# Attention's queries of two heads from seven products of quarters, with h and its sums reloaded for each group

## The chip, the cores and the metric

The kernel runs on one core of a Trainium2 chip. A core has five engines with queues of their own, each worked off strictly in order: TensorE (PE for the matmuls, PEld for its weight loads), VectorE (DVE), ScalarE (ACT), GpSimd (POOL) and SyncE (SP), which here only issues DMAs. POOL and ACT issue some too. The metric is the device time of one execution in microseconds; the lower, the better. The kernel before took 2233.8 us, the median of three runs (2233.77 to 2240.36).

## The reference

Four rows (batch entries) of 512 tokens with 512 channels pass through two layers. The first is a gated recurrence followed by Mamba-2, and another such gate followed by a mixture of experts. The second, in which the change lies, is a gate followed by grouped-query attention, and a last gate followed by a gated FFN:

```python
x = x + _L1_attn_ref(_L1_cond_ref(x, fside, fside, L1_cond_w, L1_cond_u, cond), w_q, w_kv, w_dense)
x = x + _L1_ffn_ref(_L1_cond2_ref(x, fside, fside, L1_cond2_w, L1_cond2_u, cond), ...)
```

```python
HEADS, GROUPS, KVC = (16, 4, 128)      # 4 heads to a group, HPG = 4
q = einsum('bsh,he->bse', x, w_q).reshape(b, sq, GROUPS, HPG, KVC)
kv = einsum('bsh,he->bse', x, w_kv)
k, v = split(kv, 2, axis=-1)           # each (b, sk, GROUPS, KVC)
scores = einsum('bqgpd,bkgd->bgqpk', q, k) * KVC ** -0.5
probs = softmax(where(causal, scores, -inf))
ctx = einsum('bgqpk,bkgd->bqgpd', probs, v).reshape(b, sq, HEADS * KVC)
return einsum('bse,eh->bsh', ctx, w_dense)
```

All of it is in float32. Here x is the gated input, h in the kernel.

## The kernel before, in words

**Layout.** Activations are kept transposed: channels on the 128 partitions, tokens along the free axis. h of one row is a tile of 128 x 4 x 512 floats (1 MB): four blocks of 128 channels, 512 tokens. A float32 product of 128 x 128 weights with 512 columns stands in the profile as two MATMUL records with two LDWEIGHTS.

**Stages.** In the order of time: the first layer's recurrence and Mamba-2, the mixture of experts (to about 1117 us of the profiled execution), attention (to about 1995 us), the FFN to the end.

**Attention.** The loop at the end of the attention block runs over `heads_`: for each of 4 groups, for each of 4 rows, 4 heads; 64 heads in all. `begin(n + 1)` makes the next head's queries one step ahead. For the first head of a group and row it also calls `start_group`, which makes kT (`pk`, L1630) and v (`pv`, L1638). Then `scores` makes the current head's four blocks of causal scores (`psc`, L1674). DVE masks them and takes the maximum, ACT takes the exponential (L128), DVE normalises (L1686) and transposes within blocks of 32 (L1690). Four POOL DMAs send the result to DRAM (`turned`, L1698) and one fetches it back turned (`pT`, L1716). Three heads later `settle` calls `context` (`pctx`, L1742), and after the fourth head of a row `dense` (`pd`, L1757), which DVE adds to x (L1765).

**Queries.** `queries(u, i)` is one head: four products accumulate over the four blocks of channels, and ACT scales the result into qT:

```python
pq = ps_tp("pq")
for k in range(NC):
    nc.tensor.matmul(pq, lhsT=u.wq[:, k, i * KVC : (i + 1) * KVC], rhs=u.h[:, k, :],
                     start=(k == 0), stop=(k == NC - 1))
qT = sm.tile([P, T], F32, tag="qT", name="qT")
nc.scalar.mul(qT, pq, SCALE)
```

The PSUM tag "tp" has two banks. `wq` of a group (1 MB) is loaded by `load_group` into one of two buffers; the first h (`early_h`) is made in the other one during the mixture of experts, and copied to its own place by L1617.

**h.** The four rows' h stay in SBUF for all four groups, in the four buffers of tag "h" of pool `gp`. While group 0 runs, the h of the following row is made at the third head of each row: `load_results` (`rr`, L1508, on SP) and `combine` (L1515 on ACT, L1516 on DVE, `pcb` L1521 on PE, L1525 on DVE) finish x of that row; `gated` loads the gate (L417, 1 MB) and multiplies (L406). After attention, `gated_halves` makes the FFN's h in the same buffers and splits it into a high and a low part (L1858 on ACT, L1859 on DVE). The FFN's first products (`pfg`, `pfu`, L1872 and L1873) read these.

**Other work in attention.** `nudge` spreads the last gates' recurrence (`make_gates`: `kt`, `ek`, `ekv`, scans, `eu`) over the heads, on DVE and ACT. Its loads go through SP's queue.

**Order.** A list scheduler in the programming layer sorts the instructions of all engines by its own estimates, within the program's dependencies. The queues are then fixed, and on the chip an instruction that waits holds up everything behind it on its engine. A DMA waits on its issuing engine's queue. Pools with `reuse_waits="tile"` let a new tile in old memory wait for the last user of just the tiles that lay there.

Of the kernel before, what the change touches and what calls it, by code (L numbers as in the profile page):

```python
# [10 lines left out]
F32 = mybir.dt.float32  # L11
# [72 lines left out]
def block_kernel(ctx: ExitStack, tc: tile.TileContext, a: dict, out: bass.AP):  # L84
# [61 lines left out]
    def ps_tp(name):  # L146
        return ps.tile([P, 512], F32, tag="tp", name=name, bufs=2)
# [1338 lines left out]

    def load_group(g):

        wq = wa.tile([P, NC, HPG * KVC], F32, tag="wq", name="wq")
        w = HPG * KVC  # L1490
        nc.sync.dma_start(
            out=wq, in_=a["w_q"][:, g * w : (g + 1) * w].rearrange("(k p) m -> p k m", p=P)
        )
        wkv = wa.tile([P, 2, NC, KVC], F32, tag="wkv", name="wkv")
        for i in range(2):
            c0 = i * GROUPS * KVC + g * KVC
            nc.sync.dma_start(
                out=wkv[:, i], in_=a["w_kv"][:, c0 : c0 + KVC].rearrange("(k p) m -> p k m", p=P)
            )
        return wq, wkv  # L1500

    def load_results(b, t, queue):

# [35 lines left out]
    with tc.tile_pool(name="moe_w2", bufs=1, reuse_waits="tile") as wm:  # L1539
# [18 lines left out]
        order_blocks(NEARLY, NBLK)  # L1558
        moe.know(ALWAYS)
        more(NBLK - 8)  # L1560
        first_group = load_group(0)

        more(NEARLY + FIRST + 2)
        results = {t: load_results(0, t, nc.gpsimd) for t in range(2)}
# [6 lines left out]
                results[t + 2] = load_results(0, t + 2, nc.gpsimd)  # L1571
        assert moe.i == ALWAYS + 2
        n = len(nc.cur_bb.bb.instructions)
        early_h = gated(2, 0, x[0], wa, tag="wq", name="h2_0")
        early_th = [
            i for i in nc.cur_bb.bb.instructions[n:] if i.engine == nc.scalar.engine
        ]
# [7 lines left out]


    right = dict(side="right", reuse_waits="tile")
    gp = ctx.enter_context(tc.tile_pool(name="gates", bufs=4, **right))
    with att as ph:
        wdp = ph.enter_context(tc.tile_pool(name="att_wd", bufs=1, **right))  # L1590
        sm = ph.enter_context(tc.tile_pool(name="att", bufs=2, **right))
        mp = ph.enter_context(tc.tile_pool(name="att_m", bufs=1, **right))
# [20 lines left out]
                nc.gpsimd.memset(blocks[:, :, lo:hi, :], 0.0)  # L1613
        turned_d = [dr.tile([QUAD, SQ, QUAD, SLOTS * SQ], F32, name=f"turned{i}") for i in range(4)]

        hs = [gp.tile([P, NC, T], F32, tag="h", name="h2")] + [None] * (B - 1)
        nc.sync.dma_start(out=hs[0], in_=early_h)  # L1617

        class Group:
            pass  # L1620
# [1 line left out]
        def start_group(g, b, w):  # L1622
            u = Group()
            u.g, u.b, u.ctxT = g, b, []
            u.last_row = g == GROUPS - 1 and b == B - 1
            u.wq, wkv = w
            u.h = h = early_h if (g, b) == (0, 0) else hs[b]
            pk = ps_mm("pk")
            for k in range(NC):
                nc.tensor.matmul(  # L1630
                    pk, lhsT=wkv[:, 0, k, :], rhs=h[:, k, :], start=(k == 0), stop=(k == NC - 1)
                )
            u.kT = sm.tile([P, T], F32, tag="kT", name="kT")
            nc.scalar.copy(u.kT, pk)
            pv = ps_mm("pv")
            for t in range(NT):
                for k in range(NC):
                    nc.tensor.matmul(  # L1638
                        pv[:, t * P : (t + 1) * P],
                        lhsT=h[:, k, t * P : (t + 1) * P],  # L1640
                        rhs=wkv[:, 1, k, :],
                        start=(k == 0),
                        stop=(k == NC - 1),
                    )
            u.v = sm.tile([P, NT, KVC], F32, tag="v", name="v")
            nc.scalar.copy(u.v.rearrange("p t d -> p (t d)"), pv)
            return u

        def queries(u, i):
            pq = ps_tp("pq")  # L1650
            for k in range(NC):
                nc.tensor.matmul(  # L1652
                    pq,
                    lhsT=u.wq[:, k, i * KVC : (i + 1) * KVC],
                    rhs=u.h[:, k, :],
                    start=(k == 0),
                    stop=(k == NC - 1),
                )
            qT = sm.tile([P, T], F32, tag="qT", name="qT")
            nc.scalar.mul(qT, pq, SCALE)  # L1660
            return qT

        def scores(u, i, qT):

# [109 lines left out]
                dense(old)  # L1774

        weights, dense_w = {0: first_group}, {0: load_dense(0)}
        heads_ = [(g, b, i) for g in range(GROUPS) for b in range(B) for i in range(HPG)]

        def begin(n):
            g, b, i = heads_[n]  # L1780
            if i == 0:
                if b == 0 and g + 1 < GROUPS:
                    weights[g + 1] = load_group(g + 1)
                groups[g, b] = start_group(g, b, weights[g])
            return groups[g, b], queries(groups[g, b], i)


        ffg_d = dr.tile([C, INTER], F32, name="ffg_d")
# [4 lines left out]
                es.enter_context(tc.issue_after(th))  # L1793
            act.use(act.LOG_EXP)
        look_ahead(1, (0, 1))
        groups = {}
        numbers = iter(range(GROUPS * B * HPG))
        ready, held = begin(0), []
        for n, (g, b, i) in enumerate(heads_):
            u, qT = ready  # L1800
            if g == 0 and i == 0 and b + 1 < B:
# [8 lines left out]
                nc.sync.dma_start(out=to, in_=a[name])  # L1810
            if g and b == 0 and i == 3:
                dense_w[g] = load_dense(g)
            if n + 1 < len(heads_):
                ready = begin(n + 1)
            if g == 0 and i == 2 and b + 1 < B:
                act.use(act.EXP)
                hs[b + 1] = gated(2, b + 1, x[b + 1], gp, tag="h", name=f"h2_{b + 1}")
                act.use(act.LOG_EXP)
            prs = scores(u, i, qT)
            held.append((u, prs))  # L1820
            if len(held) > 3:
                settle()
# [10 lines left out]
            act.use(act.SILU)  # L1833


    LOW = 0xFFF
    cuts = (0, 3 * P, INTER)

# [204 lines left out]
```

## Time and profile before

| | |
|---|---|
| median of three runs | 2233.8 us |
| profiled execution | 2242.7 us, span 2241.0 us, granted clock 0.981 |
| PE busy | 2135.2 us, 95% |
| DVE, ACT, POOL busy | 1526.2, 968.9, 455.8 us |
| queries `pq` on PE, 512 records | 237.4 us |
| ACT `qT` (L1660), 64 of 593 ns | 38.0 us |
| DMA | 357.38 MB, 159 GB/s on average |

A group's line in the profile gives line, engine, operation, what is written and read, the shapes and the number of instructions; then the busy time in us, the mean length of one in ns, and the engine's idle time just before them, with what ended most of it. Matmuls are pipelined, so the mean length of one (599 ns) is more than the distance from one to the next. In the timeline a line is a run of like instructions: start, length, engine, line, tiles, shapes, count, and in brackets the idle time before it with what ended that. In the view by windows each engine has its busy time and the number of instructions; the granted clock of PE (1.00 is full), the DMA engines' mean share and the GB/s follow.

### The profile page before, as it was taken

How to read it: one execution, taken by the hardware profiler on the slowest of the kernel's cores; microseconds unless marked ns; L12 is line 12 of the kernel's file. 1: busy time of each engine (PE TensorE's matmuls, PEld its weight loads, DVE VectorE, ACT ScalarE, POOL GpSimd, SP SyncE). 2: the span in 40 equal slices, each digit the busy share in tenths (PEclk: the TensorE clock that was granted, in tenths of full speed). 3: DMA queues.
4: the chain of work that ended last, by engine and by line, in shares of the span. 5: the costliest groups of instructions: out<-in, count | busy, mean ns of one | idle time of the engine just before them, and what ended most of it. 6: DMA issues, size and time to landing. Idle time of an engine off the chain costs nothing.

```text
span 2241.0 us, 23830 instructions
## 1 busy us (share of the span) xinstructions
PE 2135.2 (95%) x7570; PEld 1224.9 (55%) x7570; DVE 1526.2 (68%) x3039; ACT 968.9 (43%) x1899; POOL 455.8 (20%) x620
## 2 busy tenths in 40 slices
PE   4979999999999999999998999999999999999998
PEld 2545565565665444444454455555555555568887
DVE  8799889989653566676477766677767765555332
ACT  4576776765732234333254333333334432333221
POOL 4023242422222111222211111112112122100000
PEclk9989999999999999999989999999999999999999
DMA  7542341432424458988676555555645464531100
GB/s 257 195 132 73 107 155 67 156 122 67 167 83 141 152 190 285 382 289 285 211 252 195 179 183 150 160 164 181 185 140 175 141 195 140 185 122 38 38 20 20
DMA packets 112452, 357.38 MB, mean 159 GB/s; under 512 B 14592, under 2 KB 23168, under 8 KB 102912
## 3 DMA queue, kind: packets, MB, share of 16 engines
q1 hardware_dynamic: 78656, 224.43, 29.0%
q0 software_dynamic: 31360, 127.16, 18.9%
q10 hardware_dynamic: 2304, 4.20, 0.5%
q8 instruction: 62, 1.02, 0.2%
q14 instruction: 70, 0.57, 0.1%
HBM read 337.91 MB, written 108.00 MB: 199 GB/s over the span
## 4 chain that ended last, share of the span: by engine, by line
PE 40%; DVE 8%; ACT 1%; DMA 1%; issue 0%; DVEq 0%; ACTq 0%
PE pd L1757 10%; PE pq L1652 6%; PE pctx L1742 4%; PE psc L1674 4%; PE pk L1630 3%; PE pv L1638 3%; PE pfo L1873 2%; PE pfo L1872 2%; PE pfg L1872 2%; PE pfg L1873 2%; PE pfu L1872 2%; PE pfu L1873 2%; DVE nmax L1679 1%; DVE turned L1690 1%; DVE pr L1686 1%; DVE psc L1677 1%
## 5 line engine op out<-in xcount | busy, mean ns | idle before, releaser
L1698 POOL DMA_DIRECT2D turned<-turned x248 | 136.0, 555 | 622.8 <-DVE turned L1690 387.9
L128 ACT ACTIVATE pr<-psc,nmax 128x128 f32<-128x128 f32 (+3 forms) x256 | 134.7, 527 | 286.9 <-DVE nmax L1679 284.2
L1652 PE MATMUL pq<-h,wq 128*128 128x512 f32 x512 | 237.4, 599 | 1.8 <-DVE h L406 1.2
L1757 PE MATMUL pd<-cx,wd 128*128 128x512 f32 x512 | 222.4, 592 | 0.0
L1765 DVE TENSOR_TENSOR xr<-xr,pd 128x512 f32<-128x512 f32 x64 | 44.0, 687 | 196.8 <-PE pd L1757 196.8
L1674 PE MATMUL psc<-kT,qT 128*128 128x128 f32 (+3 forms) x512 | 160.0, 442 | 15.5 <-ACT pr L128 14.4
L1757 PEld LDWEIGHTS pd<-cx,wd 128*128 128x128 f32 x512 | 96.1, 190 | 114.8 <-issue 110.3
L1057 PE MATMUL pc<-h,wxb 128*128 128x512 f32 x320 | 145.6, 610 | 6.6 <-DVE h L406 4.0
L1652 PEld LDWEIGHTS pq<-h,wq 128*128 128x128 f32 x512 | 94.7, 193 | 102.2 <-issue 90.8
L1742 PE MATMUL pctx<-pT,v 128*128 128x512 f32 (+3 forms) x512 | 148.4, 433 | 0.0
L1742 PEld LDWEIGHTS pctx<-pT,v 128*128 128x128 f32 x512 | 96.7, 190 | 76.2 <-issue 50.5
L847 PE MATMUL po<-w,yT 128*128 128x512 f32 x296 | 134.2, 593 | 0.6 <-DMA w<-in_w2x 0.4
L814 PE MATMUL pg<-w,hT 128*128 128x512 f32 x296 | 134.2, 594 | 0.0
L825 PE MATMUL pn<-w,hT 128*128 128x512 f32 x296 | 133.4, 593 | 0.7 <-DMA w<-in_w1x 0.7
L1674 PEld LDWEIGHTS psc<-kT,qT 128*128 128x128 f32 x512 | 84.9, 191 | 74.2 <-ACT pr L128 29.7
L1679 DVE TENSOR_REDUCE nmax<-psc 128x1 f32<-128x128 f32 (+3 forms) x256 | 122.1, 481 | 2.1
L1690 DVE STREAM_TRANSPOSE turned<-pr 128x128 f32<-128x128 f32 x248 | 117.0, 493 | 1.2
L1128 PE MATMUL pz<-wzt,h 128*128 128x512 f32 x256 | 116.6, 605 | 0.3 <-ACT st L1229 0.3
L1276 PE MATMUL po<-wot,yT 128*128 128x512 f32 x256 | 115.4, 605 | 0.0
L1057 PEld LDWEIGHTS pc<-h,wxb 128*128 128x128 f32 x320 | 60.8, 195 | 78.0 <-issue 71.5
L1686 DVE TENSOR_SCALAR pr<-pr,rsum 128x128 f32<-128x128 f32 (+3 forms) x256 | 95.7, 375 | 2.2
L1677 DVE TENSOR_TENSOR psc<-psc,mask 128x128 f32<-128x128 f32 x256 | 70.9, 284 | 37.4 <-PE psc L1674 37.0
(348 smaller groups left out, 4186.3 us busy)
## 6 DMA issues: line engine op xcount, KB each, us to landing
w<-in_w1x SPq DMA_DIRECT2D x76, 1024.0 KB
turned<-turned POOLq DMA_DIRECT2D x248, 208.0 KB, 3.8
pT<-turned POOLq DMA_DIRECT2D x62, 832.0 KB, 7.3
w<-in_w2x SPq DMA_DIRECT2D x38, 1024.0 KB
wb<-in_b1x SPq DMA_DIRECT2D x38, 512.0 KB
lm<-cs SPq DMA_DIRECT2D x32, 512.0 KB
kt<-in_fT SPq DMA_DIRECT2D x62, 256.0 KB
ek<-ek SPq DMA_DIRECT2D x62, 256.0 KB
```

The source lines that it names most:

```text
L128: nc.scalar.activation(*args, **kw)
L814: nc.tensor.matmul(pg, lhsT=hT[:, k, :], rhs=self.w1[s][0][:, k, :], start=(k == 0), stop=(k == NC - 1))
L1057: nc.tensor.matmul(pc, lhsT=wxb[:, k, m * P : (m + 1) * P], rhs=h[:, k, :], start=(k == 0), stop=(k == NC - 1),)
L1652: nc.tensor.matmul(pq, lhsT=u.wq[:, k, i * KVC : (i + 1) * KVC], rhs=u.h[:, k, :], start=(k == 0), stop=(k == NC - 1),)
L1674: nc.tensor.matmul(psc[:, :n], lhsT=qT[:, qi * P : n], rhs=u.kT[:, :n], start=True, stop=True)
L1679: nc.vector.tensor_reduce(nmax, psc[:, :n], AX.X, ALU.max, negate=True)
L1690: nc.vector.transpose(blocks[:, :, 3 * qi : 4 * qi + 1, :].rearrange("p c k j -> p k c j"), pr)
L1698: nc.gpsimd.dma_start(out=d[:, :, r].rearrange("c i s -> i c s"), in_=blocks[r * SQ : (r + 1) * SQ].rearrange("i c k j -> i c (k j)"),)
L1742: nc.tensor.matmul(pctx[:, kj * P :].rearrange("p (q r j) -> p q r j", r=QUAD, j=SQ), lhsT=u.v[:, kj, :], rhs=pT[:, :, 4 * kj : 10 + kj : ...
L1757: nc.tensor.matmul(po, lhsT=dense_w[u.g][:, i, m * P : (m + 1) * P], rhs=u.ctxT[i], start=(i == 0), stop=(i == HPG - 1),)
L1872: nc.tensor.matmul(out_, lhsT=w, rhs=xs[0], start=first_, stop=False)
L1873: nc.tensor.matmul(out_, lhsT=w, rhs=xs[1], start=False, stop=last_)
```

## The change

The queries of two heads are one product of a 2 x 2 arrangement of quarters. The weights' quarters a11, a12, a21, a22 are (two blocks of channels) x (one head's 128 columns); h's quarters b11, b12, b21, b22 are (two blocks of channels) x (256 tokens); the result's quarters are (one head) x (256 tokens). Instead of eight products of quarters there are seven (p1 to p7), of four sums of weight quarters (s1 to s4, on POOL after each load) and four sums of h quarters (t1 to t4, on DVE, once for each row, tile `ht`, 1 MB). A product of quarters is two matmuls of 256 columns, so a pair of heads takes 14 of these in place of 8 of 512 columns. The results are put together by five DVE operations, two scalings on ACT and two sums on POOL, 256 columns each. One product (p3) and its DVE operation are issued after the current head's scores.

h and ht of each row are stored to DRAM in group 0 and loaded again for every group, h into two buffers, ht into one. The weights are loaded by pairs of heads (`load_pair`), one buffer for the first and one for the second pair, raw weights and sums side by side; `early_h` now takes the second pair's buffer. Pool `gp` is opened after attention instead of before it, and attention's h has a pool `hp` of its own in that place.

```diff
 def load_group(g):
-    wq = wa.tile([P, NC, HPG * KVC], F32, tag="wq", name="wq")
-    w = HPG * KVC
-    nc.sync.dma_start(out=wq, in_=a["w_q"][:, g * w : (g + 1) * w].rearrange("(k p) m -> p k m", p=P))
...
+def load_pair(g, j):
+    w = wa.tile([P, 2, NC, 2 * KVC], F32, tag=f"wq{j}", name=f"wq{j}", bufs=1)
+    c0 = (g * HPG + 2 * j) * KVC
+    nc.sync.dma_start(out=w[:, 0], in_=a["w_q"][:, c0 : c0 + 2 * KVC].rearrange("(k p) m -> p k m", p=P))
+    quads = w.rearrange("p s k (h m) -> p s k h m", h=2)
+    a11, a12, a21, a22 = (quads[:, 0, 2 * c : 2 * c + 2, h] for h in range(2) for c in range(2))
+    s1, s2, s3, s4 = (w[:, 1, i].rearrange("p (c m) -> p c m", c=2) for i in range(4))
+    nc.gpsimd.tensor_tensor(s1, a21, a22, ALU.add)
+    nc.gpsimd.tensor_tensor(s3, a11, a21, ALU.subtract)
+    nc.gpsimd.tensor_tensor(s2, s1, a11, ALU.subtract)
+    nc.gpsimd.tensor_tensor(s4, a12, s2, ALU.subtract)
+    return a11, a12, a22, s1, s2, s3, s4
...
-    early_h = gated(2, 0, x[0], wa, tag="wq", name="h2_0")
+    early_h = gated(2, 0, x[0], wa, tag="wq1", name="h2_0", bufs=1)
...
-gp = ctx.enter_context(tc.tile_pool(name="gates", bufs=4, **right))
 with att as ph:
+    hp = ph.enter_context(tc.tile_pool(name="att_h", bufs=1, **right))
...
-    hs = [gp.tile([P, NC, T], F32, tag="h", name="h2")] + [None] * (B - 1)
-    nc.sync.dma_start(out=hs[0], in_=early_h)
+    HT = T // 2
+    h_d = [dr.tile([P, NC, T], F32, name=f"h_d{b}") for b in range(B)]
+    t_d = [dr.tile([P, 4, 2, HT], F32, name=f"t_d{b}") for b in range(B)]
+    def row_tiles(b):
+        return (hp.tile([P, NC, T], F32, tag="h", name=f"h2_{b}", bufs=2),
+                hp.tile([P, 4, 2, HT], F32, tag="ht", name=f"ht_{b}"))
...
+    def mix(h, ht):
+        b11, b12, b21, b22 = quarters(h)
+        t1, t2, t3, t4 = (ht[:, i] for i in range(4))
+        nc.vector.tensor_tensor(t1, b12, b11, ALU.subtract)
+        nc.vector.tensor_tensor(t2, b22, t1, ALU.subtract)
+        nc.vector.tensor_tensor(t3, b22, b12, ALU.subtract)
+        nc.vector.tensor_tensor(t4, t2, b21, ALU.subtract)
+    def keep_row(b, h, ht):
+        nc.sync.dma_start(out=h_d[b], in_=h)
+        nc.sync.dma_start(out=t_d[b], in_=ht)
+    def load_row(b):
+        h, ht = row_tiles(b)
+        nc.sync.dma_start(out=h, in_=h_d[b])
+        nc.sync.dma_start(out=ht, in_=t_d[b])
+        return h, ht
...
-    def queries(u, i):
+    def queries(u, j):
...
+        x1, y5, u2, u3, u4 = (both(v) for v in ("x1", "y5", "u2", "u3", "u4"))   # 256 columns, one buffer each
+        p1, p6 = two()                       # two() is one bank of tag "tp", cut in halves
+        product(p1, a11, b11)
+        nc.scalar.mul(x1, p1, SCALE)
+        product(p6, s2, t2)
+        plus(u2, p6, x1)                     # DVE: SCALE * p6 + x1
+        p2, p7 = two()
+        product(p2, a12, b21)
+        plus(q[0][:, lo], p2, x1)
+        product(p7, s3, t3)
+        plus(u3, p7, u2)
+        p5, p4 = two()
+        product(p5, s1, t1)
+        nc.scalar.mul(y5, p5, SCALE)
+        product(p4, a22, t4)
+        nc.gpsimd.tensor_tensor(u4, y5, u2, ALU.add)
+        nc.gpsimd.tensor_tensor(q[1][:, hi], y5, u3, ALU.add)
+        plus(q[1][:, lo], p4, u3, -1.0)
+        yield q
+        p3, _ = two()
+        product(p3, s4, b22)
+        plus(q[0][:, hi], p3, u4)
+        yield
...
         if g == 0 and i == 2 and b + 1 < B:
-            hs[b + 1] = gated(2, b + 1, x[b + 1], gp, tag="h", name=f"h2_{b + 1}")
+            h = gated(2, b + 1, x[b + 1], hp, tag="h", name=f"h2_{b + 1}", bufs=2)
+            ht = hp.tile([P, 4, 2, HT], F32, tag="ht", name=f"ht_{b + 1}")
+            mix(h, ht)
+            keep_row(b + 1, h, ht)
+            at_hand[g, b + 1] = h, ht
+        elif i == 2 and (g, b) != (GROUPS - 1, B - 1):
+            to_g, to_b = heads_[n + HPG][:2]
+            at_hand[to_g, to_b] = load_row(to_b)
+        if b == B - 1 and i == 1 and g + 1 < GROUPS:
+            pairs_w[g + 1, 0] = load_pair(g + 1, 0)
         prs = scores(u, i, qT)
+        end_queries()                        # p3 of the pair just made
...
+gp = ctx.enter_context(tc.tile_pool(name="gates", bufs=4, **right))   # after attention
```

## The prediction

> **What bounds the kernel now.** I read the page first: engine shares, the slices in time, the costliest groups.
>
> ```profile
> span 2241.0 us, 23830 instructions
> ...
> PE 2135.2 (95%) x7570; PEld 1224.9 (55%) x7570; DVE 1526.2 (68%) x3039; ACT 968.9 (43%) x1899; POOL 455.8 (20%) x620
> ...
> L1652 PE MATMUL pq<-h,wq 128*128 128x512 f32 x512 | 237.4, 599 | 1.8 <-DVE h L406 1.2
> ...
> turned<-turned POOLq DMA_DIRECT2D x248, 208.0 KB, 3.8
> pT<-turned POOLq DMA_DIRECT2D x62, 832.0 KB, 7.3
> ```
>
> PE is the bound; the queries (pq) hold 237 us of it. The last two lines give what a DMA takes from issue to landing by size.
>
> Then the busy time by window: two short stretches just after PE had stood still, and the steady part of attention.
>
> ```profile
> 1120.00:1126.00 6.00, 5.85 (x8) 2.48 (x8) 1.99 (x3) 2.48 (x3) 0.71 (x4) 0.52 0.75 284
> 1158.00:1164.00 6.00, 5.20 (x7) 2.23 (x8) 6.00 (x14) 4.66 (x10) 2.75 (x5) 0.56 0.81 223
> 1187.00:1800.00 613.00, 603.35 (x1957) 324.26 (x1957) 446.71 (x1143) 244.76 (x584) 128.67 (x235) 1.00 0.57 171
> ```
>
> The pairs are busy us and instructions of PE, PEld, DVE, ACT, POOL; then granted clock, DMA share, GB/s. From 1187 to 1800 us PE is idle 1.6%, DVE 27%: whatever PE saves there is saved, and whatever it waits there is lost.
>
> Last, the timeline of PE: rates, the start of attention, its end.
>
> ```profile
> 1117.16 0.63 PE L1521 MATMUL pcb<-ident,rr 128*128 128x128 f32 x4 [1.53 <-DVE rr L1516]
> 1120.15 6.44 PE L1630 MATMUL pk<-h,wkv 128*128 128x512 f32 x8 [2.37 <-DVEq L1579]
> 1126.43 3.73 PE L1638 MATMUL pv<-wkv,h 128*128 128x128 f32 x32
> ...
> 1275.73 2.32 PE L1742 MATMUL pctx<-pT,v 128*128 128x512 f32 x8
> ...
> 1277.89 13.90 PE L1757 MATMUL pd<-cx,wd 128*128 128x512 f32 x32
> ...
> 1981.23 13.90 PE L1757 MATMUL pd<-cx,wd 128*128 128x512 f32 x32
> 1994.57 0.80 PE L1873 MATMUL pfu<-h_lo,ffu 128*128 128x512 f32 x1
> ```
>
> A record is half a product (each product makes two). 32 records of 512 columns take 13.90 us, 0.429 each; 32 of 128 take 3.73 us, 0.112 each. Between them a 256-column record costs 0.2175; the pctx line (two each of 512, 384, 256 and 128) fits that: 2.16 us plus a tail. The eight pk records after 1.53 and 2.37 us of idleness took 6.44 instead of 3.6 us: the granted clock was 0.52. At the end, dense (pd) and FFN follow without a gap.
>
> **The change, part by part.**
>
> *PE work.* Out: 512 records x 0.429 = 219.6 us. In: 32 pairs x 14 products x 2 = 896 records x 0.2175 = 194.9. Gain 25 us; ends 27 (0.2145, half of 0.429) and 22.
>
> *Waits for ht.* ht (1 MB, one buffer) is reloaded for 12 of the 16 rows. In the built program SP's load of the next ht waits for the last product of the row's second pair that reads the old one; PE's queue, which is in order, holds the next row's first ht product soon after. I priced the PE work between the two by the rates above: 2.37 us in six rows, 3.66 in two, 4.52 in four; together 39.6 us. No row gives the landing of this load. Nearest: in the trace the packets of h<-g, the same size on the same queue, ended 4.4 (quiet queues) to 6.4 us after issue; by the two POOL lines above 5.6 us per MB more than 208 KB, 8.3 us. I take 6.2 with the wake-ups (attention's DMA share is 0.57): 12 x 6.2 - 39.6 = 35 us. Ends: 4.7 (4.4 and the wake-ups) gives 17, 8.3 gives 60. Behind the waiting product stand the same head's third and fourth scores, then pctx and pd, so DVE and ACT run dry too and nothing makes it good.
>
> The Trainium skill (DMA: Bandwidth & Descriptors, Anatomy of one DMA) fits 2.0 us plus bytes at 436 GB/s, by which 1 MB would be 4.4 us and this term some 17 us; only the quietest load of this trace agrees, the loads in attention took 5.3 to 6.4.
>
> *Clock after the waits.* In the trace of before, after its first 30 us, PE has nine gaps of 2.4 us or more at full clock; after seven the granted clock fell to 0.5, for 3.4 us at least; of six gaps of 1.8 to 2.0 us, after four. The waits above are 1.7 to 3.8 us. A drop costs half its length, less what falls into the gap: 12 x 0.75 x 2.1 = 19 us. Ends 7 (a third of them, 1.7 each) and 41 (all, 3.4 each).
>
> The Trainium skill (TensorE: Matmul & The Clock Gate, Part 1) wants a whole idle window of about 3.4 us before the gate closes. Here 1.9 us sufficed before 1156 us. By the page only the six longest waits would count and this term would be about 10 us.
>
> *Entrance to the FFN.* Pool gp, opened after attention now, shares memory with attention's; the load of h3_0 waits for the very last pd product. Before, it was issued at 1790 us. So PE stands from the end of pd: load 4.4 to 5.5, first chunk's h 0.69 (L406), its cast 0.61 (L1858), wake-ups: 6.6 us; then PE starts at half clock and DVE feeds it (8 operations of 0.69). I take 10; ends 6.5 and 14.
>
> *Start of attention.* early_h sits in the second pair's buffer (wq1). wq1's load so waits until row 0's pk, pv and all seven products are done, 1130.0 + 28 x 0.2175 = 1136; on SP's queue, in order, three of the four rr loads of row 1 stand behind it (issued from 1122.9 before, first used by ACT at 1130.7). They land about 10 us late, and the h of row 1 with them. Ahead of them SP also waits for the SBUF copy of h (about 6 us) before h_d can be stored. wq1 lands near 1142 and its four sums on POOL (0.71 each, half of L1223's 1.43 for 512 elements) end near 1145, when the second pair could start. Of the 10 us, PE has two longer query groups (2.4 us each) as cover: I take 8; ends 0 and 14 (all of it, and a drop of the clock).
>
> *Putting quarters together.* No row has the operation. DVE: between 0.415 (L1679, 256 columns) and 0.687 (L1765, 512): 5 x 32 x 0.42 = 67 us, and 16 sums of h at 0.69, 11 us; DVE goes from 73% to about 82% in attention, below PE. ACT: 38.0 us out, 64 x 0.43 in. POOL: 64 sums of queries and 32 of weights x 0.71 = 68 us, from 21% to 29%; the scheduler put them between the DMA issues of turned, heads ahead of use. On the path: the third bank's products wait for the evacuation of the first (x1 on ACT, then u2 on DVE), with 2 to 3 us of other PE work between; where DVE is in a softmax, part shows. 32 x 0.2 = 6 us; ends 0 and 20 (one DVE operation and its queue, 0.6). If that cover goes, each pair pays 0.6.
>
> *Sums of h in group 0.* For rows 1 to 3 DVE cannot write ht until the old one is read, 2.1 us for the three sums before the first product, under 3.9 to 28 us of PE work: 3 us; ends 0 and 8.
>
> *SP and memory.* 24 loads and 8 stores of 1 MB more, and four more weight loads: 36 more issues. 32 MB over 880 us is 36 GB/s beside 171: hidden while the DMA share is 0.57; if not, the landing time above grows. The loads of h have two buffers, a row of notice: nothing. The first pair's POOL sums end before attention: nothing, else up to 3 us.
>
> Sum: -25 + 35 + 19 + 10 + 8 + 6 + 3 = +56 us on an execution of 2242.7 us (span 2241.0). It is 0.4% above the median of the runs, 2233.8; I put the same difference on the median: 2290.
>
> **Rivals.** Within 0.3% (6.7 us) nothing can be told from no change.
>
> *A. The ht loads land under cover* (ends not slower). It needs a landing within 2.4 to 4.5 us of the last read. For it: the scheduler placed the products there. Against: 208 KB took 3.8 us, and no 1 MB load less than 4.4. Waits and clock drops (54 us) go: 2290 - 54 = 2236; with the start hidden too, about 2225. It decides from landings below about 4 us.
>
> *B. Loads land as late as pT*: 60 us of waits, 30 of clock: 2290 + 36 = 2326. For it: the load of the next h is issued right behind, and pT shares the engines. Against: h<-g.
>
> *C. DVE becomes the second bound*: with 82% busy in order, each pair's evacuations cost 0.6 to 1 us: 2290 + 20 = 2310. For it: DVE is 100% busy in 1158 to 1164. Against: 73% from 1187 on.
>
> *D. The sums are not seven products*: the order of the built program shows 14 half-size products a pair, so no.
>
> **How the numbers follow.** Forecast 0.58, B 0.17, C 0.10, A 0.15 (of it 0.10 below -0.3%, 0.05 within). The forecast's own range, from the ends that are likely together (waits 25 to 45, clock 10 to 30): 2262 to 2318. For 8 in 10 I reach half into A and to the middle of B: 2240 to 2328. Faster 0.10, same 0.05, slower 0.85.
>
> **What would show it.** PE's waits in groups 1 to 3: twelve, for ht, 1.7 to 4 us each, 25 to 45 us together; a granted clock below 1.0 after most; pq records of 256 columns near 0.2175 us; one PE gap of 6 to 8 us before the first pfg; rr and h of row 1 about 10 us later. It is wrong if attention has no DMA waits on PE (then A), or if pq waits for DVE more than for DMA (C).

## The result and the profile after

The changed kernel takes 2404.4 us (median of six runs, 2396.8 to 2409.3) against 2237.5 us for the kernel before: a ratio of 1.0745, 95% interval 1.0722 to 1.0768. The direction was forecast, the size was not: 167 us more, where 56 were worked out and the range ended at 2328.

The page of the changed kernel: span, busy time, the products of the queries by what they read, and the two transfers by size.

```profile
span 2403.0 us, 25117 instructions
...
PE 2174.0 (90%) x7954; PEld 1322.4 (55%) x7954; DVE 1598.4 (67%) x3216; ACT 958.3 (40%) x1898; POOL 530.8 (22%) x716
...
L1712 PE MATMUL pq<-ht,wq 128*128 128x256 f32 x512 | 138.1, 411 | 55.3 <-DMA ht<-t_d 42.6
...
L1712 PE MATMUL pq<-h,wq 128*128 128x256 f32 x384 | 102.3, 395 | 5.8 <-DVE h L406 2.9
...
turned<-turned POOLq DMA_DIRECT2D x248, 208.0 KB, 3.9
pT<-turned POOLq DMA_DIRECT2D x62, 832.0 KB, 7.4
```

PE went from 95 to 90% busy. The two transfers land as before. The same stretch of attention as in the view by windows of before:

```profile
1187.00:1800.00 613.00, 524.99 (x1820) 323.70 (x1820) 407.46 (x1036) 197.08 (x478) 145.65 (x243) 0.92 0.55 178
```

PE was busy 603 us of the 613 before, at full clock; now 525, and at 0.92. DVE is no busier (407 us, 447 before): fewer of its instructions fit, since it stands still as well. The timeline of PE at the end of attention, beside the one shown of before:

```profile
2131.87 13.90 PE L1840 MATMUL pd<-cx,wd 128*128 128x512 f32 x32
2152.50 0.79 PE L1979 MATMUL pfg<-h_hi,ffg 128*128 128x512 f32 x1 [6.74 <-ACT h_hi L1965]
```

From the two traces the difference divides as follows (idle time is what the matmul records leave open, half clock is what the trace gives as the granted clock).

| | before | after |
|---|---|---|
| first `pk` to the end of the last `pd` | 875.0 us | 1029.2 us |
| of it, PE idle | 20.6 us | 137.1 us |
| of it, granted clock at half | 19.2 us | 157.0 us |
| first row, to its `pd` | 103.7 us | 114.2 us |
| rows of groups 1 and 2, each | 50.4 to 55.6 us | 58.8 to 68.6 us |
| from the last `pd` to the end | 245.9 us | 257.2 us |

Idleness (+116), half the added time at half clock (+69) and the saved work (-26) make 159; some of the half clock falls into the gaps, and 154 remain. So nearly all of the loss lies in attention, in every row. PE's waits name several causes:

```profile
PE pq L1712 <- DMA ht<-t_d: 42.6, 11, 5.3
PE psc L1757 <- ACT pr L128: 26.5, 22, 5.8
...
PE psc L1757 <- DVE qT L1718: 16.5, 9, 4.4
PE pcb L1534 <- DVE rr L1529: 15.1, 7, 5.0
PE pq L1712 <- ACT x L1725: 8.9, 6, 3.4
```

The columns are us in total, times, and the longest. The loads of `ht` lead, as forecast and about at the forecast size (eleven waits of 0.8 to 5.3 us, 42.6 us together; twelve and 35 us were forecast). The runs below show that this list is not a list of prices.

### The profile page after: what moved, and what is told of

Its sections match the earlier page's. It is cut to its first block, busy times and chain, and to the rows that moved or that the text cites. A ratio compares the mean times of both kernels' runs of the same rounds, so it can differ in the third digit from the quotient of the medians.

```text
span 2403.0 us, 25117 instructions
## 1 busy us (share of the span) xinstructions
PE 2174.0 (90%) x7954; PEld 1322.4 (55%) x7954; DVE 1598.4 (67%) x3216; ACT 958.3 (40%) x1898; POOL 530.8 (22%) x716
## 4 chain that ended last, share of the span: by engine, by line
PE 36%; DVE 10%; DMA 2%; ACT 2%; issue 1%; POOL 0%; DVEq 0%; ACTq 0%
PE pd L1840 9%; PE pq L1712 5%; PE psc L1757 4%; PE pctx L1825 4%; PE pk L1680 2%; PE pv L1688 2%; PE pfg L1979 2%; PE pfo L1980 2%; PE pfg L1980 2%; PE pfo L1979 2%; PE pfu L1979 2%; PE pfu L1980 2%; DVE nmax L1762 2%; DVE turned L1773 2%; DMA ht<-t_d 1%; DVE pr L1769 1%
## 5 line engine op out<-in xcount | busy, mean ns | idle before, releaser
L1757 PE MATMUL psc<-kT,qT 128*128 128x128 f32 (+3 forms) x512 | 188.7, 493 | 57.0 <-ACT pr L128 26.5
L1712 PE MATMUL pq<-ht,wq 128*128 128x256 f32 x512 | 138.1, 411 | 55.3 <-DMA ht<-t_d 42.6
L1825 PE MATMUL pctx<-pT,v 128*128 128x512 f32 (+3 forms) x512 | 159.1, 453 | 0.7 <-ACT pT L1815 0.7
L1712 PEld LDWEIGHTS pq<-ht,wq 128*128 128x128 f32 x512 | 100.6, 204 | 89.7 <-issue 30.6
L1757 PEld LDWEIGHTS psc<-kT,qT 128*128 128x128 f32 x512 | 91.2, 207 | 102.3 <-ACT pr L128 32.8
L1825 PEld LDWEIGHTS pctx<-pT,v 128*128 128x128 f32 x512 | 102.4, 201 | 72.2 <-issue 45.7
L1712 PE MATMUL pq<-h,wq 128*128 128x256 f32 x384 | 102.3, 395 | 5.8 <-DVE h L406 2.9
L1769 DVE TENSOR_SCALAR pr<-pr,rsum 128x128 f32<-128x128 f32 (+3 forms) x256 | 102.1, 401 | 1.2
```

The source lines that it names most:

```text
L1712: nc.tensor.matmul(out_, lhsT=w[:, c], rhs=xs[:, c], start=(c == 0), stop=(c == 1))
L1757: nc.tensor.matmul(psc[:, :n], lhsT=qT[:, qi * P : n], rhs=u.kT[:, :n], start=True, stop=True)
L1825: nc.tensor.matmul(pctx[:, kj * P :].rearrange("p (q r j) -> p q r j", r=QUAD, j=SQ), lhsT=u.v[:, kj, :], rhs=pT[:, :, 4 * kj : 10 + kj : ...
```

## The experiments

All times are medians beside runs of the kernel before on the same chip (2237.5 to 2249.8 us). Row times are the distance from one row's `pd` to the next's. Each edit lets the scheduler lay all queues anew; that turned out to be the point. Runs on different chips are compared by their medians, although the kernel before itself differed by 12 us between these chips.

**What is taken away: the reload, or the putting together.** Theory W: the waits for `ht` and the clock after them are the loss. Theory D: the operations that put the quarters together stand behind softmax and gate work (the recurrence that `nudge` spreads) in the queues, and hold the scores up. The first run leaves the reload out:

```diff
 def load_row(b):
-    h, ht = row_tiles(b)
+    h = hp.tile([P, NC, T], F32, tag="h", name=f"h2_{b}", bufs=2)
     nc.sync.dma_start(out=h, in_=h_d[b])
-    nc.sync.dma_start(out=ht, in_=t_d[b])
-    return h, ht
+    return h, last_ht[0]
```

> Left out: from group 1 on, the sums of h are not loaded again; all products read the sums that the last row of group 0 left (so the queries are not the reference's). The h loads stay. Theory W (PE's waits for ht, with the clock drops behind them, are the main cause): PE's 42.6 us of waits for ht go, and about half of the 138 us at half clock, so 70 to 80 us less than the changed kernel's 2404: about 2330. Theory D (the operations that put quarters together stand on DVE's queue behind softmax and gate work, and the scores wait for them; the ht waits run beside that): the waits for ht go, psc's waits for DVE qT (16.5 us) grow to 40 or more, and the time falls by less than 25: 2380 to 2404.

The second leaves the putting together out:

```diff
-nc.scalar.mul(x1, p1, SCALE)
...
-plus(u2, p6, x1)
...
-plus(q[0][:, lo], p2, x1)
+nc.scalar.mul(q[0][:, lo], p2, SCALE)
...
-plus(u3, p7, u2)
...
-plus(q[0][:, hi], p3, u4)
+nc.scalar.mul(q[0][:, hi], p3, SCALE)
```

> Left out: the putting together. The seven products are made, but four of them are scaled by ACT straight into the four quarters of the queries; no DVE and no POOL operation per pair is left (ACT has four of 256 columns instead of two). The ht loads stay. Theory W: PE still waits some 40 us for ht, with the drops of the clock, and the time falls by 10 to 25 us: about 2385. Theory D: psc's waits for DVE qT go and the rows shorten by 4 us or more each: 2340 or less.

The third has both edits:

> Left out: both, the reload of the sums and the putting together. W and D together: what is left is the seven products with h reloaded, the start and the entrance to the FFN. If the two causes are additive, the time is 2404 less the sum of the two gains; under W it is within 15 us of the run without the reload alone, under D within 15 us of the run without the putting together alone. If neither, that is above 2300, a third cause is there (the order of the products among the scores).

Measured: 2390.5 us without the reload (-14), 2289.7 without the putting together (-115), 2274.1 with both edits (-130: the two gains add up). W falls: it expected about 2330 without the reload. Its waits did go, but another took their place, as PE's waits without the reload show:

```profile
PE psc L1758 <- DVE qT L1719: 38.4, 8, 7.5
PE psc L1758 <- ACT pr L128: 20.5, 20, 2.4
PE pq L1713 <- ACT x L1726: 10.1, 11, 2.1
```

From the first row's `pd` on, the scores waited 13.6 us for the quarters with the reload and 38.4 without it. Two waits lay beside each other, and the one that ended last was named. Attention became 20 us shorter: 12 of them in two rows of group 3 (57 to 51 us each), 7 in the eight rows of groups 1 and 2. Where the putting together is left out, only 11.1 us of waits for `ht` were left, and taking them away gained 15.6 us; in the changed kernel 42.6 us of waits were worth no more.

**The entrance to the FFN.** Pools `att_h` and `att_wd` are opened in the other order, so that `h3_0` does not take the memory of `wd`.

```diff
-hp = ph.enter_context(tc.tile_pool(name="att_h", bufs=1, **right))
 wdp = ph.enter_context(tc.tile_pool(name="att_wd", bufs=1, **right))
+hp = ph.enter_context(tc.tile_pool(name="att_h", bufs=1, **right))
```

> The two pools att_h and att_wd change places in the code, so that the FFN's first h lies in memory of a row's h and not of attention's last weights of dense. W and D alike: the load of h3_0 is issued before the last dense, PE's 6.7 us before the first pfg go and most of the 9.5 us at half clock after them; 10 us less than 2404: about 2394. If the entrance was no cost of its own (something else was late beside it), less than 3 us.

2406.1 us, no change. The load is now issued at 2119 us, well before `pd` ends at 2144, but PE still waits 6.1 us: on DVE's queue the multiplication that uses it stands behind the last addition of `pd` and four operations on the FFN's weights.

```profile
2144.42 0.69 DVE L1848 TENSOR_TENSOR xr<-xr,pd 128x512 f32<-128x512 f32 x1 [2.75 <-PE pd L1840]
2145.03 0.89 DVE L1962 TENSOR_TENSOR low<-ffd 128x704 int32<-128x704 int32 x1
2145.95 2.74 DVE L1962 TENSOR_TENSOR low<-low,ffd 128x704 int32<-128x704 int32 x3
2148.61 1.28 DVE L406 SCALAR_TENSOR_TENSOR h<-th,h 128x512 f32<-128x512 f32 x2
```

In the changed kernel the load is issued at 2145.80 us, when `pd` has ended. So the 11 us at this place have two causes in a row, the memory and then the order; taking the first away shows the second.

**DVE's time, or its results?** To the run without the putting together, five operations of DVE for each pair are added back that nobody waits for:

```diff
+for i in range(5):
+    sc = sm.tile([P, HT], F32, tag=f"sc{i % 2}", name="sc", bufs=1)
+    src = q[i % 2][:, lo]
+    nc.vector.scalar_tensor_tensor(sc, src, SCALE, src, ALU.mult, ALU.add)
```

> The run in which the putting together is left out and ACT scales four of the seven products into the quarters (2289.7 us), with five operations of DVE for each pair of heads added, of the same form and size (scalar_tensor_tensor, 256 columns), which read finished quarters from SBUF and write scratch that nobody reads. So DVE has its 67 us of work back, but nothing waits for it. The queries are not the reference's. Theory D: 2290 to 2310, attention 911 to 930 us. Rival S (DVE has simply become too busy, wherever its results go): 2350 or more, attention at least 970 us.

2299.0 us: the 67 us of DVE work alone cost 9 (two executions each, 2292.9 and 2305.2 against 2288.6 and 2290.7). DVE is busy 561 us from the first row's `pd` on, as in the changed kernel (563), and attention takes 921 us instead of 1029. So it is not the amount of DVE's work; it matters that somebody waits for it, or what order follows from that. Next, the sums are taken off DVE; ACT scales and POOL adds:

```diff
-plus(u2, p6, x1)
+nc.scalar.mul(u2, p6, SCALE)
+nc.gpsimd.tensor_tensor(u2, u2, x1, ALU.add)
```

> The changed kernel with the putting together taken off DVE: ACT scales each of the seven products out of PSUM (0.38 us each), in place into the query quarters or into x1, u2, u3, and POOL makes the seven sums between them (0.7 to 1.6 us each in the trace after). Nothing is left out; the seven products, the reload of ht and the chain of sums stay. Theory D (the sums stand in DVE's queue behind softmax and gate work, and the scores wait for them): the waits of psc for DVE qT go, attention falls from 1029 us towards the 911 us of the run in which the putting together is left out; time 2290 to 2330. Rival L (the chain of dependent sums is too long on whatever engine it runs; POOL's operations are slower than DVE's): 2380 or more, with waits of psc for POOL qT of 40 us or more in place of those for DVE.

2382.7 us, near rival L and far from D as it was put: it is not DVE's queue as such. (L's sign, waits for POOL, came to 10.7 us only; PE waited 19.5 and 18.1 us for ACT to empty banks.) Then two runs on what in the operations counts. One keeps them all but not their dependence:

```diff
+c = fixed                            # a tile of zeros
...
-plus(u3, p7, u2)
+plus(u3, p7, c)
```

> The changed kernel with every operation of the putting together kept in kind, size, engine and PSUM bank (five on DVE, two on ACT, two on POOL for a pair of heads), but without their dependence on each other: DVE adds a constant tile of zeros in place of x1, u2, u3, u4, POOL adds constants into scratch, ACT writes y5 straight into its query quarter. The sums are left out, so the queries are not the reference's. Theory Q (each evacuation of PSUM stands in the queue of an engine that is behind with the softmax, and PE's next products need its bank and its quarter): 2365 us or more, as with the chain. Rival C (the chain of dependent sums is what comes late): 2290 to 2320, as without the putting together.

One gives the third bank of a pair to another PSUM tag, so that it need not wait for the first:

```diff
-p5, p4 = two()
+p5, p4 = two(ps_acc)
```

> The changed kernel with the third bank of each pair (p5 and p4) taken from the two banks of pctx and pd, so that it need not wait until the first bank (p1 and p6) is evacuated. Nothing is left out. Theory Q: 2370 or less (waits of pq for ACT x and DVE u go). If banks do not matter: 2395 to 2415, or more where pctx and pd now wait for p5 and p4.

2342.0 us without the chain, between the two expectations; 2405.6 with the other bank, no change. So the third bank's wait for the first is not the cause; waits for the other banks were not tested. The 62 us without the chain are not the price of the dependence alone, because the order of PE's queue changed with it (see the row's boundary below).

**The gate work.** It shares DVE with the softmax. These two put the gate work of groups 1 to 3 behind attention, in the changed kernel and in the kernel before:

```diff
-with after(nc.vector, nc.scalar):
-    nudge()
+if u.g == 0:
+    with after(nc.vector, nc.scalar):
+        nudge()
```

> The changed kernel with the recurrence of the last gates (kt, ek, ekv, scans, eu on DVE and ACT) not spread over the heads of groups 1 to 3, but put behind attention; group 0 is as it was. Nothing is left out. The total grows by the work put behind and is not what is read: the rows of groups 1 and 2 are (changed kernel 61.5 to 68.6 us each, before 50.4 to 55.6). Theory D (DVE's queue is late because softmax and gate work fill it): rows of 51 to 56 us, and attention near 930 us in place of 1029. Rival L (the chain itself): rows of 59 us or more.

> The kernel before with the same edit: the gate work of groups 1 to 3 put behind attention. The comparison for the run before this one: rows of groups 1 and 2 of 50 to 52 us (50.4 to 55.6 with the gate work), attention 865 to 875 us in place of 875. If attention falls by 10 us or less here and by 70 us or more in the changed kernel, the gate work cost nothing until PE had to wait for DVE.

2398.0 and 2249.1 us. The edit did not do what it says: the scheduler pulled the work forward into the first three rows of group 1, so this is no test of taking it away. What can be read: those rows became longer by more in the changed kernel (75.5 and 74.5 us) than before (56.3 and 59.8); and the rows of group 2, now without gate work, took 57.7 us on the mean against 51.3. With the gate work they took 63.5 and 52.2: of 11 us more to a row, 6 remain without any gate work in it.

**Earlier queries.** The queries of a pair are begun one head earlier:

```diff
+begin_queries(n + 2)
 if n + 1 < len(heads_):
     ready = begin(n + 1)
-if g == 0 and i == 2 and b + 1 < B:
+if g == 0 and i == 1 and b + 1 < B:
...
-elif i == 2 and (g, b) != (GROUPS - 1, B - 1):
+elif i == 1 and (g, b) != (GROUPS - 1, B - 1):
```

> The changed kernel with the queries of a pair made one head earlier, before the scores of the first head of the pair before it (in the changed kernel: before the scores of the second). h and ht of the next row and the next group's weight pairs are loaded a head earlier too; qT has four buffers, y5 goes into its query quarter. Nothing is left out. If the finished quarters come late for the scores (theory D), PE's waits of psc for DVE qT go, and the waits for ht shrink: 2290 to 2340. If it is the PSUM banks of the products, which wait for the evacuation of the bank before (theory Q): 2370 or more, with waits of pq for ACT x and DVE u of 40 us or more in place of those.

> Both edits together: queries a head earlier, and the third bank from those of pctx and pd. Theories D and Q agree that this is the fastest of the complete versions: 2270 to 2320; in no theory below the kernel before, since the start of attention, the entrance to the FFN (21 us together) and the waits for ht that remain outweigh the 25 us of PE work saved.

2303.9 us, and 2300.2 with the other bank too (two executions, 2289.3 and 2311.0, so no difference is shown). 100 of the 167 us are back with every operation in place. The edit also moved the loads: waits for `ht` fell from 42.6 to 7.0 us, which the run without the reload prices at 14 us or so. What changed is best read from DVE's waits, in attention from the first row's `pd` on; first the changed kernel, then this one.

```profile
DVE xr L1848 <- PE pd L1840: 175.3, 64, 7.3
DVE qT L1718 <- PE pq L1712: 87.4, 29, 6.3
DVE u L1718 <- PE pq L1712: 44.9, 27, 6.9
```

```profile
DVE xr L1851 <- PE pd L1843: 179.0, 59, 7.7
...
DVE u L1720 <- PE pq L1714: 10.8, 19, 2.2
DVE qT L1720 <- PE pq L1714: 6.5, 9, 2.8
```

In the changed kernel DVE, the supposedly late engine, itself stood 132 us waiting for PE's products. Before, and here, that is nothing or little (0 and 17 us).

**Thinner gate work.** On this basis, and in the kernel before, the gate work is called after three of four score blocks, so that it lasts into group 3:

```diff
-with after(nc.vector, nc.scalar):
-    nudge()
+if u.g == 0 or qi:
+    with after(nc.vector, nc.scalar):
+        nudge()
```

> The version made a head earlier (2303.9 us) with the gate work of groups 1 to 3 spread more thinly: after three of each head's four score blocks in place of all four, so that it ends in group 3 and no longer with group 2. Nothing is left out. Theory G (rows cost more than before where softmax, gate work and the putting together on DVE exceed what PE takes for the row, and nothing elsewhere): rows of groups 1 and 2 fall from 57 to 54 us on the mean, rows of group 3 rise by at most 1.5 us, attention falls by 15 to 35 us, the time to 2270 to 2292. Rival H (something else, the loads of h and ht or the turned blocks, makes groups 1 and 2 longer): attention within 8 us of 923, the time 2296 or more.

> The kernel before with the same edit: gate work after three of four score blocks in groups 1 to 3. There PE hardly waits for DVE in attention (rows of 50.4 to 55.6 us in groups 1 and 2), so theory G expects little: attention 866 to 876 us in place of 875, the time within 0.4% of before.

2303.1 us (ratio 1.0269, 1.0228 to 1.0310) and 2243.8 (1.0011, 0.9991 to 1.0031). Groups 1 and 2 gained 8 us (454.3 to 445.9), group 3 lost 10 (173.5 to 184.0). The numbers named for H came out (attention 924 us), those for G did not: it is not a matter of a few overfull rows. In the kernel before the same edit added 2 and 4 us in these places. So some of the cost moves with the gate work, but only 8 of the 35 us by which groups 1 and 2 are longer than before; what holds the rest is not shown.

**The floor.** With the queries a head earlier, the putting together moved to ACT and POOL, or left out:

> The version made a head earlier (2303.9 us) with ACT scaling all seven products out of PSUM and POOL making all seven sums. Nothing is left out. If DVE's own time is what still costs (67 us more of it than before, in rows where it is 0.8 to 0.9 busy), rows of groups 1 and 2 fall towards 53 us and the time to 2270 to 2290. If PE only waits for whichever engine empties the banks, ACT or DVE, the time stays at 2300 or above, with waits of pq for ACT in place of those for DVE.

> The version made a head earlier with the putting together left out (four of the seven products scaled by ACT into the quarters), so the queries are not the reference's. If the putting together still costs about 36 us there: 2262 to 2275. If the 36 us belong to the surroundings: within 10 us of 2304.

2327.5 us on ACT and POOL, worse than on DVE (2303.9), with 19 us of PE's waits of `pq` for ACT and v behind `pd` in eleven of fourteen rows (see below); 2254.2 without it, below the expected 2262. So 50 us of putting together remain in the version made a head earlier, and everything else costs 15 to 17 us over the kernel before; its attention takes 875.4 us, as before (875.0).

**The order at the row's boundary.** Why does DVE wait for products in the changed kernel? The timeline of PE around one row's end, before:

```profile
1535.42 3.70 PE L1630 MATMUL pk<-h,wkv 128*128 128x512 f32 x8 [0.30 <-ACT pr L128]
1538.95 3.73 PE L1638 MATMUL pv<-wkv,h 128*128 128x128 f32 x32
1542.53 1.02 PE L1652 MATMUL pq<-h,wq 128*128 128x512 f32 x2
1543.39 1.46 PE L1674 MATMUL psc<-kT,qT 128*128 128x128 f32 x6
...
1546.84 13.90 PE L1757 MATMUL pd<-cx,wd 128*128 128x512 f32 x32
1560.58 1.02 PE L1674 MATMUL psc<-kT,qT 128*128 128x512 f32 x2
```

And after:

```profile
1547.39 3.23 PE L1757 MATMUL psc<-kT,qT 128*128 128x384 f32 x4 [3.17 <-DVE qT L1718]
...
1553.47 13.90 PE L1840 MATMUL pd<-cx,wd 128*128 128x512 f32 x32
1567.20 2.74 PE L1680 MATMUL pk<-h,wkv 128*128 128x512 f32 x6
1569.78 3.73 PE L1688 MATMUL pv<-wkv,h 128*128 128x128 f32 x32
1573.35 1.03 PE L1712 MATMUL pq<-h,wq 128*128 128x256 f32 x4
1574.21 2.75 PE L1712 MATMUL pq<-ht,wq 128*128 128x256 f32 x12
1576.81 2.32 PE L1757 MATMUL psc<-kT,qT 128*128 128x128 f32 x8
```

In the program the `pd` of a row follows the third head of the next row, and that row's fourth head comes behind it, with k and v of the row after. Before, the scheduler had put that k and v ahead of `pd` (all of v in 13 of 14 rows), in seven rows some scores of the fourth head too, and scores follow right behind `pd`. After, v and all scores of the fourth head stand behind `pd` in all fourteen rows: from `pd`'s start to the next block of scores 23.3 us pass in twelve of them (13.7 in ten of fourteen before). In that stretch DVE is idle 15.7 to 19.7 us a row, against 8.8 to 14.7 before. In the rest of the row DVE is idle 2 to 9 us (1 to 12 before), while PE waits 3 to 12 (at most 3 before).

The other traces fit. In six versions v stands behind `pd` in all fourteen rows: the changed kernel, and those without the reload, with the pools swapped, with the gate work moved, with the other bank, and with the sums on ACT and POOL. They are the six slowest, 2383 to 2406 us. In all other versions of the changed kernel, 2254 to 2342 us, v is ahead in some rows or all; there belong the runs without the putting together, with idle DVE operations and without the chain, with 12 of 14 rows wholly ahead. So each of those edits changed the order as well, and its gain holds both. The test moves `pd` alone:

```diff
 if len(old.ctxT) == HPG:
-    dense(old)
+    due.append(old)
...
+def dense_due():
+    while due:
+        dense(due.pop())
...
 held.append((u, prs))
+dense_due()
 if len(held) > 3:
     settle()
```

> The changed kernel with dense (pd) of a row issued one head later, so that on PE's queue the k, v, first queries and the first scores of the next row stand ahead of it; nothing else is moved by hand and nothing is left out. Theory R (at each row's boundary PE's queue gives DVE no scores for 23.3 us, and DVE's work of the row no longer fits into what is left of it): the stretch without scores falls below 16 us, DVE's waits for pq fall from 132 to below 70 us, attention to 930 to 970 us, the time to 2305 to 2350. Rival D (the sums come late for the scores all along the row, wherever pd stands): attention within 20 us of 1029, 2385 or more.

> The version made a head earlier (2303.9 us; its stretch without scores is 14 to 15 us already) with dense one head later as well. Theory R: little left to gain at the boundary, 2285 to 2310. If more than 20 us go, DVE was still short of scores behind pd there.

2321.2 us (ratio 1.0325, 1.0235 to 1.0414) with `pd` alone moved: -83 us, and 943 us for attention, where rival D expected 2385 or more. The stretch without scores fell to 15.9 us or less in twelve of fourteen rows. What now stands ahead of `pd` are the scores of the row's fourth head, not the next row's as the expectation has it. With queries a head earlier as well: 2288.7 us (1.0180, 1.0111 to 1.0249), 15 us less than with these alone, the lowest median of a complete version, and still slower than the kernel before. DVE's waits with `pd` moved:

```profile
DVE xr L1848 <- PE pd L1840: 91.9, 36, 7.3
DVE qT L1718 <- PE pq L1712: 67.4, 30, 7.2
DVE u L1718 <- PE pq L1712: 33.6, 26, 5.1
DVE psc L1760 <- PE psc L1757: 33.5, 30, 2.1
```

The waits for products fell less than expected (132 to 101 us, below 70 was said), those for `pd` fell instead (175 to 92), which fits the fourth head's scores standing ahead of `pd` now. Among these versions with DVE's putting together, the sum of the waits orders the length of attention:

| DVE waits in attention for | `pd` | `pq` | scores | attention |
|---|---|---|---|---|
| before | 194 | 0 | 35 | 875 us |
| after | 175 | 132 | 13 | 1029 us |
| without the reload of `ht` | 178 | 117 | 15 | 1009 us |
| no chain | 192 | 30 | 33 | 963 us |
| `pd` a head later | 92 | 101 | 34 | 943 us |
| queries a head earlier | 179 | 17 | 23 | 923 us |
| both | 98 | 59 | 41 | 912 us |

After against before: 91 us more of waiting, and 50 more of work (563 us against 513), make up 141 of the 144 us that attention is longer from the first row's `pd` on. The order is not proof of a cause: DVE's work is much the same in all these versions (559 to 569 us), so the length is work plus waiting. It also has an exception outside the table (queries a head earlier with the other bank, 232 us of waits, 927 us).

**What stays open.** With every sum in place, moving `pd` gives back 83 us, earlier queries 100, both 116; how the rest divides between the order, the late sums and the gate work is not shown. Why the scheduler puts v behind `pd` was not tried. And the putting together still costs about 35 us in the best version (2288.7 against 2254.2 without it and with `pd` where it was); the runs do not put this down to one operation or engine.

## Why the prediction was wrong, step by step

- *PE work, -25.* Right. A record of 256 columns came every 0.216 us, one of 512 every 0.429: 896 x 0.216 = 193.5 against 219.6, a gain of 26.
- *Waits for ht, +35, and the clock after them, +19.* Right as waits (eleven, 42.6 us), wrong as a price. The loads took longer than the 6.2 us assumed: from issue to the first product behind such a wait 5.3 to 11.8 us passed, 7.3 at the median. The 4.4 us from the Trainium skill's fit are further off, and its section (DMA: Bandwidth & Descriptors, Anatomy of one DMA) gives them for the path of GpSimd's DMAs, while SP issues these. Without the reload 14 us were gained; without the putting together the reload was worth 15.6 (2289.7 to 2274.1). The terms came to 54 together, the measured price to 14 to 16 (20 in attention alone). The clock term was too small for another reason: stretches at half clock followed the waits of every kind, 138 us more of them, at up to half their length. The error in the waits was the sentence that DVE and ACT run dry too and nothing makes it good: DVE was busy in 39.1 of the 42.6 us (ACT in 19.4), and where these waits were taken away PE waited for the quarters instead.
- *Entrance to the FFN, +10.* 11 us measured, with the one wait of 6.7 us. The reason given, the memory of `gp`, is only half of it.
- *Start of attention, +8.* The first row took 10.5 us longer, and `pcb` waited 15.1 us for `rr`. The size came out, but by luck: `rr` was 6 to 9 us late and h of row 1 about 6 (10 were forecast). In the run without the putting together they were 6 to 8 and 4 us late, and the first row took only 1 us longer than before (104.7 against 103.7 us). Most of the 10.5 us go with the putting together.
- *Putting quarters together, +6, ends 0 and 20.* This is the step that failed: taken out, it was worth 115 us, 3.6 a pair instead of 0.2. It was priced at each pair, by the operation that might wait, with 2 to 3 us of other PE work as cover and DVE's average share (82%, below PE) as the reason that little would show. That average hid that DVE is nearly full in one part of the row and idle in another. The runs showed in its place a cost of the order at the row's boundary, where the built order has v and the fourth head's scores behind `pd`: with every sum kept, 83 us came back when `pd` alone was moved, and 100 when the queries were begun a head earlier. The rest, the chain of the sums and the work beside softmax and gate work, is not divided further. That order was there to be read before the run, as that of `ht` was.
- *Sums of h in group 0, +3.* Not separated; the rows of group 0 (61 to 68 us) are no longer than those of groups 1 and 2.
- *Rivals.* A did not happen. B's landing was nearly right (7.3 us at the median, 7.8 on the mean, against 8.3), but not its price. C came nearest with a sixth of the price, but its reason, DVE too busy as a whole, does not hold: with the same DVE work and nobody waiting for it the time was 2299.0 us. D, that the sums are not seven products, was rightly excluded. The sign named for C, that `pq` waits more for DVE than for DMA, did not show although the sums were the dearest part: the wait appeared on the other side, as DVE waiting for PE, and on the scores.
- *The range.* The ends named for it (waits 25 to 45, clock 10 to 30) give 2271 to 2311 with the other terms as they stand, not 2262 to 2318; the difference is not explained.
- *The premise* that whatever PE saves in this stretch is saved did not hold either: the 26 us saved were lost in PE's idle time, 116 us more than before.

## What to carry to other kernels

When two engines feed each other through in-order queues, price a change by the order of one whole period, not by the waits of single operations: write down when in the row each engine has work, and ask of every new dependence which stretch of it becomes idle. A list of one engine's waits names who came last, not what would be gained; look at the other engine's waits for the first as well, and add them. Saved work on the bounding engine is worth nothing until the order lets the second engine finish its row in the time that remains.

## What was not expected of the hardware

The granted clock falls in units. In the changed kernel's attention the 26 stretches at half clock last 3.41 us (10 of them), 6.83 (12) or 10.24 (4), one, two or three times the same length, 157.0 us together. And short gaps can suffice: of PE's gaps at full clock, 19 of 20 of 2.5 us or more were followed by one, all four of 2.0 to 2.5, five of six of 1.6 to 2.0, two of six of 1.2 to 1.6, one of six of 0.8 to 1.2. It is not the gap alone: in the version made a head earlier with thinner gate work only one of eight gaps of 1.6 to 2.0 us was, and several of the short gaps counted here lie within 3 us of another.

Counted by windows the rule is sharper. In each of the twenty traces all changes of the granted clock lie on a grid of 3.413 us, to within 0.01 us. Of the windows of this grid at full clock in attention, all twenty traces together, half clock followed on 217 of 217 in which PE was idle 2.0 us or more in all by its matmul records, on 38 of 93 with 1.6 to 2.0 us, and on 1 of 4763 with less. Of the 217, 28 held only gaps below 1.6 us each. So it is the idle time within a window that counts, from about half of it on, whether it is one gap or several.

The Trainium skill (TensorE: Matmul & The Clock Gate, Part 1) has a window of 3413 ns that runs freely, and the half clock after at least one idle window. The unit of 3.41 us agrees; that a whole window must be idle does not, by the windows above.
